# Layer 0's two-tile block of sums: mask operands of two source tiles, half the side steps, and the vector steps spread over layer 1's products

## The chip, the cores and the metric

The kernel runs on one core of one Trainium2 chip. The metric is the device time of one execution, in microseconds; the figure for a kernel is the median of its runs. A profile comes from one execution of its own, whose time is given beside the runs.

## What is computed

Four graph layers are applied to 2708 nodes with 512 features, each followed by a residual addition and a layer norm. The stage that is changed belongs to layer 0 and to the start of layer 1:

```python
# layer 0
keep    = Ab & (cumsum(Ab, axis=1) <= 64)        # first 64 neighbours of each node
nb_sum  = keep @ X                               # 2708 x 2708 by 2708 x 512
nb_mean = nb_sum / max(keep.sum(1), 1)
xj = leaky_relu(nb_mean @ W_nb.T + b_nb)
xi = leaky_relu(X @ W_line.T + b_line)
x  = layernorm(x + xi + where(cnt > 0, xj, 0))
# layer 1
agg = mask @ x / max(deg, 1)
out = relu(concat([x @ W_self + b_self, agg @ W_nb + b_nb]) @ W_comb + b_comb)
x   = layernorm(x + out)
```

Layers 2 and 3 are graph attention, and layer 3 ends in a small feed-forward part. Their instructions are not touched by the change.

## The kernel before

The nodes are 22 tiles of 128 rows, the last one with 20 rows. Layer 0 multiplies X by W_nb first (y = X W_nb), keeps y as a rounded high half and a low half (`yH`, `yL`), and then sums the kept neighbours' rows of y on TensorE. This sum is the matmul of line 609: for a destination tile t and a source tile j, the stationary operand is a 128 x 128 piece of the transposed mask, and the moving operand is `yH` or `yL` of source tile j with 512 columns. The last source tile has one half alone, so a destination tile takes 43 matmuls.

The destination tiles are worked in six blocks: `cuts` is (20, 22), (0, 4), (4, 8), (8, 12), (12, 16), (16, 20). The first block has two tiles, 86 matmuls, and the others four tiles, 172 matmuls. For each source tile j of a block, `kept` (lines 467 to 471) has ScalarE make the fp32r operand `kT` from the mask, which is held as one-byte values: 256 columns for the two-tile block, 512 for the others. `kT` has two buffers and is made one source tile ahead of the matmuls.

The transposed mask is not complete when this stage starts. Masks of the first 14 destination tiles (in the order of `cuts`) were made earlier. The other 8, numbered 14 to 21, are made while the sums run, by the generator `other_masks` (lines 474 to 512). A mask goes through these operations: a load from HBM on GpSimd's queue, a count on ScalarE over all 2708 columns (line 317), four parts of a running sum and product on VectorE (lines 323 and 326) that keep the first 64 neighbours, one DMA transpose on SyncE's queue (line 344), four sign operations on ScalarE that put it into the mask's array (line 349), and a small copy of its last rows (line 354). The generator gives up control at 98 places: five at first, then eleven per mask, and five at the end.

Two more generators follow it in one chain called `both`. `weights1` (lines 538 to 571) multiplies layer 1's weights W_self and W_nb by the two halves of W_comb: a tile of the weight is loaded, transposed on TensorE (line 139), copied (line 141), multiplied (line 299) and copied out (line 561), with a bias part on VectorE. `vectors` (lines 574 to 594) makes 24 attention vectors for layers 2 and 3: each step loads a 256 KB slice of a weight, multiplies it on VectorE (line 592) and reduces it (line 593).

The chain is advanced once per source tile j of each block, 132 times in all, and each step's instructions are issued behind the making of the next `kT`. What is left is done at once after the blocks. A second generator, `finish` (lines 520 to 535), carries a block's sums to the end of layer 0 during the next block: bias (line 524), leaky ReLU (line 229), an accumulating transfer that adds x to a row buffer (line 528), the sum (line 530), the layer norm (lines 121 to 128) and the stores. Its last instance runs during layer 1's products.

These products (lines 628 to 645) follow the blocks. For each tile they take x W_nb' (whose halves are kept by lines 271 and 276) and x W_self' plus a bias (line 643), store the latter (line 644), and rewrite one tile of the mask as 0 and 1 on VectorE (line 637).

[...] The order within the stage is what the loop issues, with `issue_after` naming an instruction behind which a step is to stand.

## Time and profile before

| | us |
|---|---|
| median of 3 runs | 2889.34 |
| lowest and highest run | 2887.77 and 2891.82 |
| the profiled execution | 2882.82 |
| its span, first to last instruction | 2881.0 |
| TensorE busy in the span | 2805.4 |
| VectorE, ScalarE, GpSimdE busy | 1996.1, 1525.6, 292.4 |
| first matmul of the six blocks | 190.05, 221.92, 263.62, 305.05, 350.12, 409.84 |
| first of layer 1's products | 462.41 |

In the profile a row names line, engine, operation, the output and inputs by the program's names, and the shape. A number in square brackets behind a row of the timeline is the time for which its engine was idle before it, and the instruction that ended this. PEld is the load of the stationary operand, which overlaps PE. SPq and POOLq are the queues' own times for issuing DMAs.

### The profile page before, as it was taken

The numbers are of one execution on the slowest core, as the hardware profiler recorded it, in microseconds if no ns is written. First come the engines' busy times: TensorE is split into PE (matmuls) and PEld (weight loads), VectorE is DVE, ScalarE is ACT, GpSimd is POOL, SyncE is SP. The second block draws the span as 40 slices with busy tenths as digits, with TensorE's granted clock in tenths as the row PEclk, the third lists the DMA queues.
The fourth block names the chain that finished last, engine by engine and source line by source line (L and its number), as shares of the span: only waits on it lengthen the run. The fifth ranks groups of instructions, "written<-read, shape, count | busy, mean of one in ns | idle before, by whom it ended". The sixth has DMA issues, their size and how long they took to land. (4 is left out here: it accounts for less than half of the span.)

```text
span 2881.0 us, 35689 instructions
## 1 busy us (share of the span) xinstructions
PE 2805.4 (97%) x13910; PEld 1552.4 (54%) x13910; DVE 1996.1 (69%) x2364; ACT 1525.6 (53%) x1749; POOL 292.4 (10%) x458
## 2 busy tenths in 40 slices
PE   9999999999999999999999999999999999999998
PEld 5457765458887434444466443444375555555565
DVE  6867747543335999999978999999954435445342
ACT  4646533223235999999955999999950000000011
POOL 2112221211120000000021000000200010100001
PEclk9999999999999999999999999999999999999999
DMA  7746647423323011111152111110161000000000
GB/s 169 150 106 136 155 128 183 128 71 125 109 85 78 28 37 37 35 54 40 35 161 101 38 38 41 49 44 34 35 170 55 4 26 15 26 15 16 15 19 25
DMA packets 203686, 202.64 MB, mean 70 GB/s; under 512 B 126855, under 2 KB 151756, under 8 KB 203508
## 3 DMA queue, kind: packets, MB, share of 16 engines
q1 hardware_dynamic: 167592, 122.05, 15.7%
q0 software_dynamic: 24912, 74.01, 9.3%
q10 hardware_dynamic: 11004, 4.22, 0.6%
q8 instruction: 111, 1.82, 0.3%
q14 instruction: 67, 0.55, 0.1%
HBM read 137.90 MB, written 55.66 MB: 67 GB/s over the span
## 5 line engine op out<-in xcount | busy, mean ns | idle before, releaser
L867 DVE SCALAR_TENSOR_TENSOR e<-v_bc,ucol,maskT 128x1408 f32<-128x1408 f32 (+3 forms) x798 | 1133.1, 1483 | 315.0 <-PE pn L1268 307.1
L896 ACT ACTIVATE c<-e,bcol 128x1300 fp8e4<-128x1300 f32 (+2 forms) x688 | 956.5, 1412 | 61.7 <-DVE e L867 16.2
L1068 PE MATMUL po<-e,R 128*64 128x512 f32 (+3 forms) x4224 | 893.8, 548 | 25.5 <-DVE e L867 23.4
L1068 PEld LDWEIGHTS po<-e,R 128*64 128x64 f32 (+1 forms) x4224 | 333.2, 136 | 553.1 <-issue 389.9
L1268 PE MATMUL pn<-e,R 128*128 128x512 f32 (+1 forms) x1008 | 396.3, 557 | 0.8
L1268 PEld LDWEIGHTS pn<-e,R 128*128 128x128 f32 x1008 | 177.5, 190 | 195.9 <-issue 181.5
L1197 ACT ACTIVATE w<-pl,b 128x256 f32<-128x256 f32 (+1 forms) x88 | 41.0, 466 | 365.6 <-PE pl L1195 365.6
L126 POOL TENSOR_TENSOR ln_rs<-ln_rs,half 128x1 f32<-128x1 f32 (+1 forms) x88 | 55.5, 631 | 1281.0 <-DVE ln_rs L125 1263.0
L609 PE MATMUL acc<-yH,kT 128*128 128x512 f32 x418 | 170.3, 407 | 5.8 <-ACT kT L470 4.4
L788 PE MATMUL pm<-w,xT 128*128 128x264 f32 (+1 forms) x704 | 163.9, 387 | 2.6 <-issue 0.9
L609 PE MATMUL acc<-yL,kT 128*128 128x512 f32 x418 | 163.6, 391 | 0.0
L659 PE MATMUL acc<-yH,mf 128*128 128x512 f32 x418 | 162.7, 389 | 0.0
L659 PE MATMUL acc<-yL,mf 128*128 128x512 f32 x418 | 162.6, 389 | 0.0
L1195 PE MATMUL pl<-lin 128*128 128x256 f32 (+1 forms) x704 | 152.9, 371 | 0.6 <-DVE lin L1097 0.6
L1220 PE MATMUL pl<-lin,w 128*128 128x512 f32 x336 | 150.8, 593 | 0.0
L1195 PEld LDWEIGHTS pl<-lin 128*128 128x128 f32 x704 | 129.3, 190 | 31.2 <-issue 15.8
L656 ACT CAST mf<-maskT 128x1024 fp32r<-128x1024 fp8e4 (+1 forms) x66 | 64.6, 978 | 151.7 <-PE acc L659 144.8
L788 PEld LDWEIGHTS pm<-w,xT 128*128 128x128 f32 (+1 forms) x704 | 129.7, 190 | 27.9 <-ACT xT L141 2.4
L299 PE MATMUL pm<-w,xT 128*128 128x512 f32 x288 | 131.9, 601 | 6.4 <-DVE yL L276 5.8
L470 ACT ACTIVATE kT<-maskT 128x512 fp32r<-128x512 fp8e4 (+1 forms) x132 | 77.6, 593 | 98.5 <-PE acc L609 98.3
L968 PE MATMUL pd<-c,parts_c 128*12 128x384 fp8e4 (+2 forms) x2688 | 128.3, 307 | 0.0
L299 PE MATMUL pm<-weight,xT 128*128 128x512 f32 (+1 forms) x256 | 118.2, 605 | 0.6 <-DVE u L643 0.6
(280 smaller groups left out, 2783.7 us busy)
## 6 DMA issues: line engine op xcount, KB each, us to landing
v_bc<-v_dram SPq DMA_DIRECT2D x16, 704.0 KB
x_dram<-u POOLq DMA_DIRECT2D x42, 256.0 KB, 2.5
v_bc<-v_dram SPq DMA_DIRECT2D x16, 650.0 KB
m<-in_adj_dram POOLq DMA_DIRECT2D x13, 677.0 KB, 7.1
rows<-in_x_dram SPq DMA_DIRECT2D x21, 256.0 KB
r_dram<-u POOLq DMA_DIRECT2D x21, 256.0 KB, 3.5
rows<-r_dram SPq DMA_DIRECT2D x21, 256.0 KB
rows<-in_x_dram POOLq DMA_DIRECT2D x21, 256.0 KB, 4.7
```

The source lines that it names most:

```text
L299: order(nc.tensor.matmul(pm[:m], xT[:, k, :m], w[:, k, :], start=(k == 0), stop=(k == KD - 1)))
L470: made = nc.scalar.activation(kT[:, :w], maskT[:, j, b[0] * P:b[0] * P + w], AF.Relu, scale=-1.0)
L609: nc.tensor.matmul(pa[t], kT[:, (t - b[0]) * P:(t - b[0] + 1) * P], y(j), start=(j == 0 and y is yH), stop=(j == LAST))
L659: nc.tensor.matmul(pa, mf[:, j - g0, :], y(j), start=(j == 0 and y is yH), stop=(j == LAST))
L788: nc.tensor.matmul(pm[a][:m, :D // 2 + heads], xT[:, k, :m], w[:, k, a, :D // 2 + heads], start=(k == 0), stop=(k == KD - 1))
L867: self.made = nc.vector.scalar_tensor_tensor(e[:, :w], v[:, :w], ucol[:, j, h:h + 1], maskT[:, j, c0:c0 + w], op0=OP.max, op1=OP.mult)
L896: nc.scalar.activation(c[:, :w], e[:, :w], AF.Sigmoid, bias=bcol[:, j, h:h + 1], scale=STEP, saturate=False)
L968: pe(nc.tensor.matmul(p[32 * g:32 * g + 12, :c1 - c0], parts_c[:, j, h, :], c[:, c0:c1], start=(i == 0 and h == hs[0]), stop=(i == NT - 1 ...
L1068: pe(nc.tensor.matmul(po[i][HO * k:HO * k + HO, :c1 - c0], R2[at, j, h * HO:(h + 1) * HO], e[at, a:a + c1 - c0], start=(i_ == 0), stop=(i_ ...
L1195: nc.tensor.matmul(pl[:, :w], self.lin1[:, k, f * P:(f + 1) * P], h[:, k, :w], start=(k == 0), stop=(k == KD - 1))
L1220: nc.tensor.matmul(pl[:n], gT[:, f, (t - t0) * P:(t - t0) * P + n], self.lin2[:, f, :], start=(f == 0), stop=(f == KF - 1))
L1268: nc.tensor.matmul(pn[k][:, :w], R2[at, j, k * P:(k + 1) * P], e[at, :w], start=(j == 0), stop=(j == NT - 1))
```

## The change

In `kept` the operand covers as many source tiles as fill 512 columns: two in the two-tile block, one in the others. It returns a list of the pieces, and the loop makes the next operand only when the list is used up. In the two-tile block the chain `both` is advanced at odd j alone, eleven times instead of 22. What is left of the chain after the blocks is not done at once: each tile of layer 1's products takes two steps, between the transposes of the next tile and the product with W_self.

```diff
             def kept(b, j):
                 w = (b[1] - b[0]) * P
-                kT = st.tile([P, 4 * P], F32R, name="kT", bufs=2)
-                made = nc.scalar.activation(kT[:, :w], maskT[:, j, b[0] * P:b[0] * P + w], AF.Relu, scale=-1.0)
-                return kT, made
+                g = 4 * P // w
+                kT = st.tile([P, 4 * P], F32R, name="kT", bufs=2).rearrange("p (g n) -> p g n", g=g)
+                made = nc.scalar.activation(kT, maskT[:, j:j + g, b[0] * P:b[0] * P + w], AF.Relu, scale=-1.0)
+                return [kT[:, i, :] for i in range(g)], made
...
-            kT, nxt_made = kept(cuts[0], 0)
+            nxt, nxt_made = kept(cuts[0], 0)
+            kTs = []
             for i, b in enumerate(cuts):
                 ts_ = range(*b)
                 pa = {t: sums() for t in ts_}
                 for j in range(NT):
-                    if j + 1 < NT:
-                        nxt, nxt_made = kept(b, j + 1)
-                    elif i + 1 < len(cuts):
-                        nxt, nxt_made = kept(cuts[i + 1], 0)
+                    if not kTs:
+                        kTs = nxt
+                        after = j + len(kTs)
+                        if after < NT:
+                            nxt, nxt_made = kept(b, after)
+                        elif i + 1 < len(cuts):
+                            nxt, nxt_made = kept(cuts[i + 1], 0)
+                    kT = kTs.pop(0)
                     for t in ts_:
                         for y in halves(j):
                             nc.tensor.matmul(pa[t], kT[:, (t - b[0]) * P:(t - b[0] + 1) * P], y(j),
                                              start=(j == 0 and y is yH), stop=(j == LAST))
-                    kT = nxt
                     if j % 3:
                         next(todo, None)
-                    with tc.issue_after(nxt_made.ins):
-                        next(both, None)
+                    if i or j % 2:
+                        with tc.issue_after(nxt_made.ins):
+                            next(both, None)
...
-            for _ in both:
-                pass
...
                 if t + 1 < NT:
                     xTs(t + 1)
+                for _ in range(2):
+                    next(both, None)
                 pm = product(xT, n, wself, 1)
```

## The prediction

> **What bounds the kernel now.** I read the page's totals first, then the instructions of L609 (the sums of layer 0), then a table of 10-us windows over that stage, then the timeline where a window falls short. The page, busy time by engine and two groups (busy us, mean ns | idle before, releaser):

> ```profile
> PE 2805.4 (97%) x13910; PEld 1552.4 (54%) x13910; DVE 1996.1 (69%) x2364; ACT 1525.6 (53%) x1749; POOL 292.4 (10%) x458
> L609 PE MATMUL acc<-yH,kT 128*128 128x512 f32 x418 | 170.3, 407 | 5.8 <-ACT kT L470 4.4
> L470 ACT ACTIVATE kT<-maskT 128x512 fp32r<-128x512 fp8e4 (+1 forms) x132 | 77.6, 593 | 98.5 <-PE acc L609 98.3
> ```

> TensorE is busy 97% of the span, so only its gaps are to be had. The chain that ended last is 0% everywhere and tells nothing. All gaps of L609, in us and times:

> ```profile
>   ACT kT L470: 9.8, 10
>   ACT u L622: 1.3, 2
> ```

> So the whole stage has 11.1 us of gaps. The windows (PE busy is the first number after the length) show where:

> ```profile
> 190.00:200.00 10.00, 10.00 (x36) 5.92 (x36) 1.96 (x3) 4.02 (x8) 3.67 (x8) 1.00 0.74 149
> 200.00:210.00 10.00, 8.43 (x36) 6.33 (x35) 7.57 (x8) 5.28 (x11) 1.73 (x2) 1.00 0.32 70
> 210.00:220.00 10.00, 5.37 (x22) 3.79 (x21) 8.02 (x8) 5.94 (x9) 0.93 (x2) 1.00 0.39 73
> ...
> 340.00:350.00 10.00, 7.67 (x26) 5.55 (x24) 5.08 (x12) 5.00 (x9) 1.13 (x2) 0.83 0.93 226
> ```

> Two of them lie in the two-tile block (190.05 to 221.92) and one in the third of the four-tile blocks (305.05 to 350.12). The timeline of the first (start, length, row):

> ```profile
> 199.12 2.54 ACT L317 ACTIVATE spare<-spare,gate 128x2708 bf16<-128x2708 bf16 x1
> 202.10 0.50 PE L609 MATMUL acc<-yH,kT 128*128 128x512 f32 x1 [1.57 <-ACT kT L470]
> 211.29 2.54 ACT L317 ACTIVATE w<-w,gate 128x2708 bf16<-128x2708 bf16 x1
> 214.28 0.50 PE L609 MATMUL acc<-yH,kT 128*128 128x512 f32 x1 [1.57 <-ACT kT L470]
> ...
> 218.04 1.06 ACT L349 ACTIVATE maskT<-weight 128x1024 fp8e4<-128x1024 bf16 x1 [3.51 <-DMA weight<-spare]
> 219.46 2.54 PE L609 MATMUL acc<-end,kT 128*128 128x512 f32 x6 [3.06 <-ACT kT L470]
> ```

> A count of 2.54 us stands on ScalarE between two kT; with two tiles a kT feeds four matmuls (4 × 0.2275 = 0.91 us), and two buffers cover less than the count. The last gap is the sign of mask 14, which waits for its DMA transpose with the next kT behind it. The three gaps are 6.2 us; from start to start the matmuls there are 1.95, 1.95 and 3.45 us apart where 0.2275 is usual, so the block loses 6.7. The other place, in the four-tile block:

> ```profile
> 338.61 3.36 SPq L344 DMA_TRANSPOSE weight<-spare  x1
> 342.08 0.51 SPq L205 DMA_DIRECT2D rows<-r_dram  x1
> 343.82 1.06 ACT L349 ACTIVATE maskT<-weight 128x1024 fp8e4<-128x1024 bf16 x1 [4.14 <-DMA weight<-spare]
> 345.45 4.60 PE L609 MATMUL acc<-end,kT 128*128 128x512 f32 x12 [2.33 <-ACT kT L470]
> ```

> The same chain: VectorE's scans came late, so the transpose was issued late, and sign, kT and matmul follow, 338.61 to 345.45 = 6.84 us from issue to resumed PE. A count in a four-tile block costs only 0.21 us, since a kT there feeds 8 matmuls, 1.82 us.

> [...] a ready kT stands behind the count and the sign, and PE idles 1.57 and 3.06 us. [...] the load of rows at 342.08 goes out after the 3.36 us of the transpose ahead of it on SP.

> **The change, part by part.** The sum is made against the profiled execution, 2882.8 us (span 2881.0 and 1.8 around it); the median of runs, 2889.3, is 6.5 above it, and I add 6.5 at the end.

> 1. *kT of two source tiles in the two-tile block.* 22 operations of 0.42 us become 11 of 0.63: 9.2 to 6.9 us of ScalarE, worth nothing by itself, as ScalarE waits for PE there (98.3 us over the stage). What counts is that each now covers 8 matmuls, 1.82 us, as in the other blocks. The number of matmuls stays 86.

> 2. *Half the steps in that block.* The mask steps, weight steps and vector steps form one list, of which 22 were taken there and now 11. Of five lead steps and eleven per mask only the count of mask 14 falls in this block, behind the kT of tiles 12 and 13; neither the count of mask 15 nor the sign of mask 14 is there any more. The remaining count costs what it costs in a four-tile block: kT 0.63 + count 2.54 + its read 0.1 + kT 0.63 = 3.9 us against two kT's work of 3.64, about 0.25. So 6.7 − 0.25: **−6.5** (between −5 and −7).

> 3. *The list is 11 steps later everywhere after.* In the order of the built program, signs fall behind kT 8 and 19 in each four-tile block, as before but for the other mask: mask 14 behind kT 8 of the first, 15 behind 19, and so on to 19 behind kT 19 of the third, 20 behind kT 8 of the fourth, 21 behind kT 17 of the fourth. Blocks 1 and 2 had no wait for a sign in these places before: 0. Block 3 had 2.33 us for a sign of that place and has the same vector work: 0. In block 4 mask 21's sign is new. It is the last mask, so its signs follow its transpose after three steps instead of waiting for another mask's scans, and stand two kT earlier than a usual sign. PE reaches kT 18 at 18 × 1.82 = 32.8, + 1.0 at the block's start, + 0.2 for the count, + 1.7 for the clock drop that falls on it (the drop near 346 us; it is fixed in time and no cost of the change) = 35.7 us after the block's first matmul. The transpose goes out when VectorE has the four scans, which stand behind the 4-tile finish of the block before, as in block 3: there 338.61 − 305.05 = 33.6 us after its first matmul, and PE resumed 40.4 after it. I walk block 4 to 34.2 and 41.0. So 40.4 to 41.0 against 35.7, a wait of 4.7 to 5.3: **+5** (between 0, if VectorE is not late, and +9).

> 4. *First layer-1 weight.* Two of the four transposes of the first W_self tile stand in TensorE's order in block 4 after 56 matmuls, while their load stands on SP behind the transpose of mask 20, a load of r0, the 1 MB W_comb load, and a buffer freed by the finish of the third block. I put its landing at 17 to 18 us after the block's start and PE's arrival at 14.7: 2 to 4 us of wait, but before kT 18, so it is contained in the 5 us above: PE comes to kT 18 later and waits there less. **0**, and if item 3's wait is not there, up to +3.5. Otherwise the 29.4 us of PE work of the weights move from blocks 4 and 5 to block 5; their count is the same.

> 5. *Vector steps spread.* Before, 9 steps of the list were left over after the blocks and taken at once; now about 20, two a tile. A vector step is a multiply of 0.69 and a reduction of 0.68, 1.37 us of VectorE. By the built order 21 of 24 fall into layer 1's products (15 before), in the first ten tiles (before: five). A tile is about 7.25 us of PE. VectorE has per tile 0.69 (yL) + 0.69 (u) + 1.62 (mask) + one finish step, mean 1.7, = 4.7; two vector steps make 7.4 us, at the limit for ten tiles, where three made 8.8 for five before. PE's idle there before is this:

> ```profile
> PE pm L299 <- DVE yL L276: 5.8, 4, 1.9
> ...
> PE pm L299 <- DVE u L643: 0.6, 1, 0.6
> ```

> The overload goes from 5 × 1.5 = 7.7 to 10 × 0.15 = 1.5 us by the mean, but the waits for the accumulating transfers (VectorE u L530, 11.3 us, up to 5.1 each) stay and now meet a full VectorE four times instead of an idle one later. I take **−0.5** (between −4 and +8.2, the last if all six added steps of 1.37 land on PE). The loads of the vector steps move with them; two buffers let each go out a step ahead, behind the products' loads on SP.

> Sum: −6.5 + 5 + 0 − 0.5 = −2.0. 2882.8 − 2.0 = 2880.8; with 6.5, **2887.3 us**.

> **The rivals.** *A, the forecast, gained in block 0 and given back in block 4:* 2885 to 2890.5. For it: the same chain stalled in block 3 at 345.45 with the same vector work. *B, not given back:* VectorE reaches the scans of mask 21 in time, because no next mask's scans compete. Then −6.5, with −0.5 to −3 from the products: 2880 to 2882.8. For it: before, mask 21's sign stood early in a block and cost nothing. Against: this is after one step's wait for r0 loads queued on SP behind a transpose. *C, slower:* layer 1's products become bound by VectorE. Place: the first ten tiles; price: 6 × 1.37 = 8.2 us, and 6 × 2.5 = 15 if each step also waits for its 256 KB load (15 steps at about 2.5 us apart before). It decides from the point where VectorE's 7.4 us per tile exceeds PE's 7.25 by 0.8 or more over ten tiles. With A's −1.5 it gives 2896 (2895 to 2903). Against: in those products the multiplies waited for W only 4.1 us in all before. *D, the change does not do what it says:* the count in block 0 still stops PE, because the pair's kT waits for both halves. Gain 2 to 3, give-back 5: 2891 to 2893.

> **How the numbers follow.** A 0.50, B 0.25, C 0.15, D 0.10. From no change a measurement of this kernel tells 0.2%, 5.8 us: faster is below 2883.5, slower above 2895.1. B gives 0.23 of faster and A 0.05 with its low end and the runs' spread (4 us); C gives 0.13 of slower and D 0.01; the rest is the same: 0.28, 0.58, 0.14. The range runs from B's 2879.5 to C's near end, 2896.5, which leaves some 0.1 above and 0.05 below. A's own range is 2885 to 2890.5.

> **What would show it.** Item 1 and 2: kT rows of 128x512 only, no PE gap over 0.4 us and one count between the first and last matmul of the two-tile block, which takes about 24.5 us (86 × 0.2275 = 19.6 and 4.2 of products in it) instead of 31.9. Item 3: one gap of 2 to 6 us before kT 18 of block 4, with a sign waiting for the DMA transpose; no such gap would be B. Item 4: a gap in front of the transposes of W_self (L139) in block 4. Item 5: the idle before layer 1's products by yL and u stays at 3 to 8 us. Wrong would make it: gaps over 12 us in those products, new waits of PE for W_self in block 5, or a shift in the later layers, whose instructions are the same and whose times I take as unchanged.

## The result and the profile after

The changed kernel took 2878.84 us (median of 6 runs, 2877.88 to 2880.78) against 2888.89 for the kernel before (6 runs): a ratio of 0.9966, 95% interval 0.9953 to 0.9979. Measured again beside more runs of the kernel before it was 0.9978 (0.9970 to 0.9987), 6.4 us faster; the ratios are of means, the medians differ by 5.6. The two intervals overlap between 0.9970 and 0.9979, 6 to 9 us. The forecast was 2887.3 us, 1.6 less than the median before; the range began at 2879.5.

The page after, totals and the two groups of the sums (line numbers are one to six higher):

```profile
PE 2803.0 (97%) x13910; PEld 1552.0 (54%) x13910; DVE 1995.0 (69%) x2364; ACT 1523.8 (53%) x1738; POOL 293.8 (10%) x458
L615 PE MATMUL acc<-yH,kT 128*128 128x512 f32 x418 | 171.4, 410 | 3.8 <-ACT kT L471 2.3
L471 ACT ACTIVATE kT<-maskT 128x512 fp32r<-128x512 fp8e4 x121 | 75.5, 629 | 100.7 <-PE acc L615 99.4
```

There are 121 operands of one shape instead of 132 of two. The gaps of all matmuls of the sums, in us and times, went from 11.1 to 5.7 us:

```profile
  ACT kT L471: 4.2, 9
  ACT u L628: 1.5, 3
```

The windows of 10 us, with PE's busy time the first number after the length and PEclk, the granted clock, third from the right:

```profile
200.00:210.00 10.00, 9.79 (x43) 7.75 (x42) 5.85 (x7) 5.64 (x8) 1.73 (x2) 1.00 0.30 56
210.00:220.00 10.00, 10.00 (x46) 8.00 (x45) 9.25 (x16) 4.81 (x8) 0.00 (x0) 1.00 0.43 80
220.00:230.00 10.00, 9.79 (x44) 7.78 (x43) 7.28 (x10) 7.42 (x9) 6.10 (x9) 1.00 0.91 198
330.00:340.00 10.00, 8.09 (x29) 5.82 (x28) 5.17 (x6) 5.78 (x10) 2.38 (x4) 0.83 0.86 159
350.00:360.00 10.00, 6.67 (x26) 5.06 (x25) 8.62 (x18) 5.00 (x7) 7.87 (x10) 0.86 0.82 259
```

The two-tile block has no hole over 0.21 us left, and no half-speed stretch follows it: before, the granted clock was 0.50 from 219.94 to 223.36 us. The third four-tile block still has its wait for a sign, now of mask 19, and the fourth has a hole that was not there before. The timeline of both:

```profile
328.30 3.32 SPq L344 DMA_TRANSPOSE weight<-w  x1
335.19 4.30 PE L615 MATMUL acc<-end,kT 128*128 128x512 f32 x12 [1.91 <-ACT kT L471]
...
352.14 0.33 SPq L205 DMA_DIRECT2D rows<-in_L_gnn_W_self_dram  x1
356.06 0.44 PE L139 MATMUL ps_tr<-ident,rows 128*128 128x128 f32 x2 [3.33 <-DMA rows<-in_L_gnn_W_self_dram]
...
370.05 5.31 SPq L344 DMA_TRANSPOSE weight<-w  x1
378.91 0.50 PE L615 MATMUL acc<-yH,kT 128*128 128x512 f32 x1 [0.80 <-ACT kT L471]
```

TensorE waits 3.33 us for the load of W_self's first tile, and then 0.80 for mask 21's sign. There are two profiles of each kernel, so the stage can be cut up (us from the first matmul of each block to that of the next; the fifth four-tile block ends with its last sum, and the products run from there to the first matmul of layer 1's sums). The 462.41 in the table of the kernel before is that end; the first product starts at 462.25.

| | before | before again | changed | changed again |
|---|---|---|---|---|
| two-tile block and first four-tile block | 73.6 | 74.2 | 64.9 | 65.0 |
| second | 41.4 | 41.4 | 41.4 | 41.4 |
| third | 45.1 | 45.1 | 44.1 | 43.1 |
| fourth and fifth, with the weights | 112.3 | 112.8 | 118.3 | 119.0 |
| layer 1's products | 161.2 | 162.1 | 160.0 | 158.7 |
| the whole stage | 433.5 | 435.5 | 428.7 | 427.0 |
| from there to the last matmul with `groups` (L1225, after L1229), 3.6 us before the last of all | 2242.2 | 2250.9 | 2244.1 | 2245.8 |

By the means, −8.9, 0, −1.5, +6.1 and −2.3: the stage gains 6.65 us. The last row differs by 8.7 us between two executions of one and the same kernel. It holds layers that the change does not touch, and a difference of this size is enough to account for how differently profiled executions and medians stand to each other.

### The profile page after: what moved, and what is told of

It reads as the page before. It is cut to its first block, busy times and chain, and to the rows that moved or that the text cites. A ratio compares the mean times of both kernels' runs of the same rounds, so it can differ in the third digit from the quotient of the medians.

```text
span 2877.4 us, 35676 instructions
## 1 busy us (share of the span) xinstructions
PE 2803.0 (97%) x13910; PEld 1552.0 (54%) x13910; DVE 1995.0 (69%) x2364; ACT 1523.8 (53%) x1738; POOL 293.8 (10%) x458
## 3 DMA queue, kind: packets, MB, share of 16 engines
q8 instruction: 111, 1.82, 0.3%
## 5 line engine op out<-in xcount | busy, mean ns | idle before, releaser
L663 PE MATMUL acc<-yL,mf 128*128 128x512 f32 x418 | 162.6, 389 | 0.0
L299 PE MATMUL pm<-w,xT 128*128 128x512 f32 x288 | 130.1, 594 | 6.2 <-DVE yL L276 5.5
L471 ACT ACTIVATE kT<-maskT 128x512 fp32r<-128x512 fp8e4 x121 | 75.5, 629 | 100.7 <-PE acc L615 99.4
L299 PE MATMUL pm<-weight,xT 128*128 128x512 f32 (+1 forms) x256 | 117.5, 602 | 1.3 <-DVE u L647 1.3
```

Of the source, the lines that this page charges most:

```text
L299: order(nc.tensor.matmul(pm[:m], xT[:, k, :m], w[:, k, :], start=(k == 0), stop=(k == KD - 1)))
L471: made = nc.scalar.activation(kT, maskT[:, j:j + g, b[0] * P:b[0] * P + w], AF.Relu, scale=-1.0)
L663: nc.tensor.matmul(pa, mf[:, j - g0, :], y(j), start=(j == 0 and y is yH), stop=(j == LAST))
```

## The experiments

Each ratio is to runs of the kernel before on the same chip. "Stage" is the second last row of the table above, from one profile; between two profiles of one kernel it differed by 1.7 and 2.0 us. The diffs are against the changed kernel unless the text names another, and "..." stands for lines left out.

**The kernel before, once more.** No edit.

> The kernel before, profiled once more. Its first profile (2882.8 us) lies 6 us below all six of its runs (2887.2 to 2891.8), while the profile of the changed kernel (2879.2) lies among its runs. Theory 1, the first profile was a favourable execution: span now near 2887, and the stage that is longer by 6 us names what the first profile hid; if it is layers 2 and 3 the change has no part in it, if it is the blocks of sums or layer 1's products the change removed waits that the first profile did not show. Theory 2, the profiler itself makes this kernel faster: 2881 again in the profile, 2888 in the runs.

Measured: 2893.2 us in the profile, 1.0005 (0.9997 to 1.0013) in the runs. Theory 1 in its first form (later layers): the stage is 2.0 us longer than in the first profile, and the layers after it 8.7. The profiler does not make the kernel faster. So the 6.5 us that the prediction added to its profiled execution were right as an amount, and belonged for the most part to later layers.

**Parts of the change.** Third part alone:

```diff
-                g = 4 * P // w
+                g = 1
...
-                    if i or j % 2:
-                        with tc.issue_after(nxt_made.ins):
-                            next(both, None)
+                    with tc.issue_after(nxt_made.ins):
+                        next(both, None)
```

> Only the third part: the 9 steps left over are taken two a tile in layer 1's products instead of at once; operands of one source tile and all 22 steps in block 0 as before. My theory (the gain is block 0's): within 2 us of before, blocks equal, the products' first gap (1.9 us at the second tile) gone and later ones longer. Rival (the products are where the 10 us of the medians lie): 4 to 8 us faster.

Measured: 0.9997 (0.9989 to 1.0006), stage 436.9. My theory held: no gain. The first gap in the products is still there (2.05 us), so that detail of it was wrong; the products take 163.4 us, no less than before.

First part alone (the loop over the blocks as in the last diff, what is left taken at once after the blocks, `g` as in the change):

```diff
-                for _ in range(2):
-                    next(both, None)
...
+            for _ in both:
+                pass
```

> Only the first part: operands of two source tiles in block 0; 22 steps there, the rest at once after the blocks. My theory: the two gaps of 1.57 us at the counts shrink to about 0.3 each, the gap of 3.06 at the sign of mask 14 stays near 3 because the transpose lands when it did; block 0 shorter by 3 us, all else equal: 3 us faster. Rival (the sign's gap goes too, since a pair gives more cover): 5.5 us faster.

Measured: 0.9996 (0.9988 to 1.0004), stage 433.9, the first two blocks 73.3 us against 73.6 and 74.2. The rival's 5.5 us are out; my 3 us stand at the edge of the interval, but the gap at the sign did not stay as it was. From the timeline:

```profile
211.56 3.60 SPq L344 DMA_TRANSPOSE weight<-spare  x1
216.86 2.00 ACT L349 ACTIVATE maskT<-weight 128x1024 fp8e4<-128x1024 bf16 x2 [4.17 <-DMA weight<-spare]
219.43 0.80 PE L615 MATMUL acc<-yH,kT 128*128 128x512 f32 x1 [5.02 <-ACT kT L471]
```

The two gaps at the counts have shrunk to 0.21 and 0.49 us, and the gap at the sign has grown from 3.06 to 5.02: TensorE comes earlier to a sign that waits 4.17 us for the DMA of its transpose. About 1 us of this growth is the pairing's own doing. Two sign operations (2.00 us) now stand on ScalarE ahead of the next operand, where one (1.06) stood before. Better cover alone buys waiting time here; the paired operands pay when the sign is also taken out of the block.

Second and third part without the first:

```diff
-                g = 4 * P // w
+                g = 1
```

> Second and third part without the first: half the steps in block 0 and the rest spread, operands of one source tile. My theory: one count with four matmuls of cover, a gap of 1.6 us, no sign: block 0 shorter by 5 us; block 4 longer by 4 us as in the changed kernel (3.3 before W_self's transposes, 0.8 before an operand of the sums): 1 to 2 us faster in the profile, and 1.4 slower than the changed kernel. Rival (the paired operands carry the gain): no faster than before.

Measured: 0.9988 (0.9982 to 0.9995), 3.5 us faster, stage 431.6; 3 us short of the changed kernel. One gap of 1.59 us at the one count (207.65), then W_self's load with 3.89. The theory held, except that the gain was larger than I had it. The first two blocks are 6.3 and 6.9 us shorter, with no half-speed stretch near 220 us any more.

First and second part without the third (`for _ in both: pass` after the blocks, nothing in the products):

> First and second part without the third: the 20 steps left over, all vector steps among them, are done at once between the blocks and layer 1's products. Theory (the spread is needed once the half steps leave 20 behind): block times as in the changed kernel; 20 vector steps of 1.4 us of VectorE stand ahead of the first yL, so the first products wait: 10 to 25 us slower than the changed kernel, with one gap of 10 us or more. Rival (the builder lets the products' VectorE work pass): within 2 us of the changed kernel.

Measured: 0.9990 (0.9983 to 0.9997), stage 431.7. Neither: no gap of 10 us, but the products take 162.6 us against 158.7 to 160.0 with the spread. So the third part is worth some 3 us once the second has left 20 steps over (3.1 by the medians, 2.6 to 3.9 in the products), and nothing by itself.

**The changed kernel again.** No edit.

> The changed kernel once more, beside its variants. Theory: from the first matmul of the sums to the first of layer 1's sums it takes 429 us in the profile against 433 to 436 before, and the rest of its gain in the medians (10 us) is the spread of executions in later layers; so with more runs the gain is 6 to 8 us, a median near 2880.5. Rival: the gain of 10 is real, 2878.5.

Measured: 2882.27 us against 2887.89, 0.9978 (0.9970 to 0.9987), stage 427.0. The theory's gain of 6 to 8 us agrees with the 6.4 of the ratio, whose interval is 3.8 to 8.7 us and leaves out the rival's 10.

**W_self's transposes out of block 4.**

```diff
-                            nc.tensor.matmul(pa[t], ...
+                            held = nc.tensor.matmul(pa[t], ...
...
-                        with tc.issue_after(nxt_made.ins):
+                        with tc.issue_after(nxt_made.ins), tc.issue_after(held.ins):
                             next(both, None)
```

> The changed kernel with TensorE's instructions of the side steps held behind the sums of their step: W_self's first transposes leave block 4 and stand in block 5. Theory, as the prediction's item 4 had it: the wait of 3.3 us disappears and the wait for mask 21's sign at the operand of source tile 18 grows from 0.8 to 4, so no change, within 1 us. Rival (the load's wait is a cost of its own): 3 to 5 us faster than the changed kernel, with a sign wait of 1 us or less.

Measured: 0.9988 (0.9980 to 0.9996), 3 us slower than the changed kernel beside it; stage 431.8. Timeline:

```profile
372.15 6.22 SPq L344 DMA_TRANSPOSE weight<-w  x1
379.89 1.06 ACT L349 ACTIVATE maskT<-weight 128x1024 fp8e4<-128x1024 bf16 x1 [9.06 <-DMA weight<-w]
381.52 0.80 PE L615 MATMUL acc<-yH,kT 128*128 128x512 f32 x1 [7.79 <-ACT kT L471]
```

The load's wait is gone and the sign's wait took it over, as the theory said, but with 7.79 us instead of 4. The block began at 339.84, so TensorE resumed 41.7 us into it; with the load's wait in place that was 39.6 and 40.3. The transpose went out 32.3 us into the block, against 30.7 and 31.6, and took 7.7 us from issue to the sign that it released, against 7.2 and 7.0. Half speed then lasted from 376.2 to 386.4 us, 10.2 us instead of 3.41; behind the wait the sums stood 0.43 us apart (382.11 to 383.82) where 0.2275 is usual. Near 357 us, where the changed kernel has a stretch behind the load's wait, they stood 0.2275 us apart (355.66 to 365.40).

**The last mask's signs later as well.** As the last one, and, at the end of `other_masks`,

```diff
+                for _ in range(2):
+                    yield
                 for _ in left:
                     yield
```

> As hold, and the last mask's signs two steps later (behind the operand of source tile 19 or 20 of block 4), everything behind them in the list two steps later too. Theory: neither wait is left (the transpose lands about 39.6 us after the block's start, TensorE reaches operand 20 at about 40), nor the drop of the clock behind the 3.3 us; block 4 takes about 42 us instead of 46.7, 4 to 6 us faster than the changed kernel. Rival (VectorE's backlog only moves the wait into block 5 or the products): same as the changed kernel.

Measured: 1.0001 (0.9992 to 1.0009), stage 432.2. The rival came: block 4 shrinks to 45.1 us but keeps a sign wait of 2.52, block 5 grows from 71.6 to 73.1, and the products have waits of 3.38 and 2.99 us.

**TensorE filled while it waits.** In the kernel before (`held` is the last matmul of the step):

```diff
+                    fill = {(0, NT - 3): 8, (3, NT - 3): 4}.get((i, j), 0)
+                    if fill:
+                        filler = ps_mm.tile([P, D], F32, name="pm1")
+                        with tc.issue_after(held.ins):
+                            for _ in range(fill):
+                                nc.tensor.matmul(filler, yH(0)[:, :P], yH(0), start=True, stop=True)
```

> The kernel before with filler matmuls on TensorE, where it waits for a sign anyway: 8 (1.82 us) ahead of the operand of source tile 20 in the two-tile block, 4 (0.91 us) ahead of that of source tile 20 in the third four-tile block; their results are not used. Theory: the half-speed stretches of 3.4 us at 219.9 and 346.2 us follow from the idle time [...]; with the waits of 3.1 and 2.3 to 2.6 us cut to about 1.3 and 1.5 both stretches vanish, though no wait ends earlier: blocks one and two together 73.6 to 74.2 us before, now 1.5 to 2 less, block four 45.05, now about 43.4, the run 3 us faster. Rival (the stretches come at their own times, as the prediction took them): they stay near 220 and 346 us and the run takes as long as before.

Measured: 0.9992 (0.9984 to 1.0000), 2.3 us faster than before; stage 431.3, the first two blocks 72.3, the third four-tile block 43.1. Windows of about 3.41 us each, the length of one half-speed stretch, in the kernel before:

```profile
216.30:219.80 3.50, 0.44 (x3) 0.30 (x3) 3.43 (x3) 1.76 (x3) 0.93 (x2) 1.00 0.37 69
219.80:223.30 3.50, 3.50 (x9) 2.24 (x8) 2.79 (x4) 3.48 (x8) 0.54 (x1) 0.52 0.95 156
342.80:346.20 3.40, 1.07 (x5) 0.67 (x4) 1.28 (x2) 2.38 (x3) 0.28 (x1) 1.00 0.71 176
346.20:349.60 3.40, 3.40 (x9) 2.65 (x9) 3.40 (x9) 2.22 (x6) 0.63 (x1) 0.51 1.05 308
```

and with the filler:

```profile
216.30:219.80 3.50, 3.02 (x14) 2.03 (x12) 3.43 (x3) 2.38 (x4) 0.94 (x2) 1.00 0.31 39
219.80:223.30 3.50, 3.04 (x13) 1.64 (x11) 3.40 (x5) 3.36 (x7) 0.54 (x1) 1.00 0.98 180
342.80:346.20 3.40, 3.00 (x13) 2.18 (x12) 3.39 (x7) 3.23 (x6) 0.91 (x1) 1.00 0.99 313
346.20:349.60 3.40, 2.76 (x11) 1.55 (x11) 3.37 (x7) 3.03 (x7) 0.54 (x1) 1.00 0.38 71
```

Both half-speed stretches are gone: the granted clock is 1.00 where it was 0.52 and 0.51, with 9 matmuls in such a stretch before and 11 to 13 now. So these two followed from TensorE's waits of 3.06 and 2.33 us, and the rival is out.

What a stretch costs is less sure than that. The sums also resumed 0.8 us (two-tile block) and 1.0 us (third four-tile block) earlier after the start of their block than in the first profile of the kernel before, because the transposes went out that much earlier, which the filler does not explain. From there to the end of the first four-tile block it took 0.6 and 1.1 us less than in the two profiles of the kernel before, and to the end of the third 1.0 and 0.7. That is less than the 1.7 us estimated as half of a stretch's 3.41 us. A wait that is missing behind a stretch is a part of this: in the kernel before, the sums wait 0.64 us for u at 263.62 and 305.05, the starts of the second and third four-tile blocks, and not at 350.12, behind the stretch that ends at 349.65.

**VectorE's backlog out of the way.** In the third and fourth four-tile blocks of the changed kernel, two of four tiles' finish behind the last scan of the mask that is worked there (`scanned` holds it):

```diff
-                    if j % 3:
-                        next(todo, None)
+                    if j in (1, 2, 4, 5, 7, 8, 14, 16, 17, 18, 20, 21) if i in (3, 4) else j % 3:
+                        with tc.issue_after(scanned[0].ins) if i in (3, 4) and j >= 14 else nullcontext():
+                            next(todo, None)
```

> The changed kernel with the second half of the finish steps (two of its four tiles) in the third and fourth four-tile blocks put behind the last scan of the mask that is worked there. Theory: VectorE's backlog is what makes the transposes late; with 5 us of it out of the way the sign waits (1.3 to 1.9 us in the third, 0.8 to 1.1 in the fourth block) go, the wait for W_self's load (3.3 to 3.7) and its half-speed stretch stay: 2 to 3 us faster than the changed kernel. Rival (the transpose's own length, 7 us there, or the queue on SyncE holds the sign): same.

Measured: 1.0007 (0.9999 to 1.0016), stage 436.3. In the third block the sign's wait is gone (41.4 us here and in the next run, against 43.1 and 44.1), so the backlog is its cause. But in the fourth, which began at 335.48:

```profile
352.03 0.69 ACT L631 ACTIVATE u<-acc,rkeep 128x512 f32<-128x512 f32 x1 [14.40 <-DVE ln_st L121]
352.77 0.79 PE L617 MATMUL acc<-yH,kT 128*128 128x512 f32 x1 [13.43 <-ACT u L631]
```

The sums leave PSUM into four buffers u, and the one of a tile whose finish was put off was not free. A wait of 1 to 2 us was gone, and one of 13 had come.

With TensorE's side instructions held too:

> As pause, and TensorE's side instructions held as in hold, so that W_self's first transposes are out of block 4. Theory: neither wait is left in block 4, no half-speed stretch: block 4 at 42 us or less instead of 46.7 to 47.4, the run 5 to 7 us faster than the changed kernel. Rival: as in hold, the sign of mask 21 takes over the wait, 4 us or more, and the run is no faster than the changed kernel.

Measured: 1.0005 (0.9996 to 1.0014), stage 438.4, the same wait with 14.15 us. What the backlog costs in block 4 is not settled by these two, as the new wait hides it.

**One vector step per tile.**

```diff
-                for _ in range(2):
-                    next(both, None)
+                next(both, None)
```

> The changed kernel with one vector step per tile of layer 1's products instead of two, so that they last over nearly all 22 tiles. My theory (item 5 of the prediction: VectorE's 7.4 us per tile against TensorE's 7.25 makes the products wait): with one step it is 6.1, the products' waits of 6.2 to 6.8 us fall to 3 to 4, and from the first product to layer 1's sums it takes 156 us instead of 158.7 to 160.0: 3 us faster than the changed kernel, a median near 2879 to 2880 against 2887.5 before. Rival (the waits come from the chains through accumulating transfers, not from the vector steps): no change in the products, the same as the changed kernel within 1 us.

Measured: 0.9999 (0.9991 to 1.0007), products 163.5 us, stage 431.7. The theory falls: with fewer vector steps per tile the products wait no less (for yL and u seven gaps, 8.1 us, the longest 2.24 behind u and followed by a half-speed stretch; 6.8 and 5.4 us in the changed kernel). So the mean load is not what sets them. How the steps fall between the other VectorE work may, but this is not shown: the chain that sets those gaps was not taken apart, and the rival fits the result but was not tested by itself.

None of these variants measured faster than the changed kernel.

## Why the prediction was wrong

The prediction favoured no change (within 0.2%), and its range began 0.7 us too high for the first measurement. The sum was −2.0 us, and the stage gained 6.65. The miss of 4.6 us is the sum of four terms: −2.4 in the first two blocks, −1.5 in the third four-tile block, +1.1 in the fourth and fifth, −1.8 in the products. The step that failed is the pricing of TensorE's waits by their own length. The prediction left the half-speed stretch at 219.94 us out of the sum, and called the one near 346 "fixed in time and no cost of the change". The filler shows that the waits ahead brought both about: with matmuls in them the granted clock stayed at 1.00. The other mis-sized term, of the same order, is that of the products, and its cause is open. By its own steps:

1. *Two-tile block, −6.5.* Right in mechanism and place: no count's wait, no sign. Mis-sized: with the first four-tile block, into which the cost ran on, it was −8.6 and −9.2. Of the missing 2.1 to 2.7 us some 1.7 are the stretch at 219.94 us, estimated as half of its 3.41 us, since the matmuls that stand there now have no gaps. In the changed kernel, without the wait, there is none near 220. The prediction's own figures had this remainder. Its −6.5 would leave 25.4 of the block's 31.9 us, yet it forecast 24.5, and 24.0 came. The 86 sums take 19.6 us, the eight products 3.6 (not 4.2), the gaps 6.7: 2.0 of the 31.9 are left, of which 1.0 is the part of the stretch that lies in the block.

2. *Third four-tile block, 0.* It was −1.0 and −2.0: the wait for the sign was 1.91 and 1.32 us instead of 2.33 and 2.60, and in one of the two profiles no half-speed stretch followed.

3. *Fourth block, +5.* The give-back came: +6.1 by the means for the fourth and fifth blocks. TensorE resumed at the operand of source tile 18 at 39.6 and 40.3 us, forecast 40.4 to 41.0. Here too the stretch (357.1 and 356.5 us, behind the wait for the load) is a cost of the wait: without it the sums stood 0.2275 us apart there. The prediction had counted 1.7 us of half speed on this way, but for the drop near 346; that one did not come, and the one that came has another cause. This part of the agreement is luck.

4. *W_self's load, contained in item 3.* It released TensorE 16.7 and 17.1 us into the block, forecast 17 to 18, and held it for 3.3 and 3.7. TensorE came at 13.4 and not at 14.7; and 17 to 18 less 14.7 is 2.3 to 3.3, not 2 to 4. That the sign would take over if the load did not wait is shown by the run that took the transposes out, which is even slower. That loads stand behind a transpose which waits on SyncE's queue is shown better than by the prediction's line by the queue's own waits: between 190 and 470 us of the kernel before its transposes waited 97.8 us for VectorE there.

5. *Products, −0.5.* It was −2.3. The waits for yL and u fell from 6.4 and 8.6 us to 6.8 and 5.4, by the means 1.4 less:

```profile
PE pm L299 <- DVE yL L276: 5.5, 5, 2.1
PE pm L299 <- DVE u L647: 1.3, 2, 0.8
```

One of the two profiles of the kernel before has a half-speed stretch in the products (472.5 us, behind a wait of 1.88), neither of the changed kernel has one; that is 0.9 us of the mean, estimated as half of 1.7. The picture of a load of 7.4 us of VectorE against 7.25 of TensorE is not what rules there (one step per tile changed nothing for the better); the size of −0.5 rested on it. What rules is open.

A's mechanism was right and its total wrong: the give-back came in full, and yet the total is B's or better, because the first two blocks and the products gained more than A had for them. C did not come: the products became shorter. D did not come: no gap in the two-tile block is over 0.21 us. The ends of the ranges are not all of one piece (B's low end is 2880 and 2879.5, C's near end 2895 and 2896.5), which changes nothing here.

The step from profile to median was sound as a number, but both it and the first measurement's 10 us lean on later layers, which vary by 9 us between executions; the repeated 6.4 us agrees with the 6.65 of the stage.

## What to carry to other kernels

## What the runs showed of the hardware

The clock. In the profile of the kernel before, TensorE's granted clock was 0.50 for 3.41 us from 219.94, 346.24 and 472.53 us, behind waits of 3.06, 2.33 and 1.88 us, and for 6.83 us from 90.24, behind one of 3.55. In that of the changed kernel it was 0.50 for 3.41 us from 90.86, 336.62 and 357.10, behind waits of 3.55, 1.91 and 3.33. Else it was below 1.00 behind the last matmul alone. From 219.94 to 223.36 us 9 matmuls were at work, and 16 in the 3.44 us behind it, at 1.00.

The length of a wait alone did not tell whether a stretch followed. In the kernel before, a wait of 2.06 us that ended at 2108.93, in a layer that the change does not touch, had none behind it, nor had waits of 2.15 (to 495.28) and 1.95 (to 2104.70) in the changed kernel, though those of 1.88 and 1.91 had. What decided was not shown. The waits come from modelled ends of matmuls; the author's estimate is that they are good to some tenths.

The DMA transpose of one mask took 5.2 us from issue to the sign in the third block of the kernel before (338.61 to 343.82), with 3.36 us on SyncE's queue. In the fourth block of the changed kernel, where it went out 30.7 us into the block and a sign waited for it, it took 7.2 us (370.05 to 377.28), with 5.31 on the queue; in the run with W_self's transposes out of that block, 32.3 us into it, 7.7 us with 6.22. What it shared the DMA engines with was not varied.
